# Feed-forward ends on Trainium2: weights prepared earlier, four row groups normalised by GpSimd, the last constant added by DMA

## The chip, the core and the metric

The kernel runs on one core of one Trainium2 chip. The metric is the device time of one launch in microseconds (us), lower is better. Instructions go to five engines that run side by side: PE (TensorE, matrix products), DVE (VectorE), ACT (ScalarE), POOL (GpSimd) and SP (SyncE, which only issues transfers). ACT and POOL can issue transfers as well. Every engine works through its own list in order, and waits for the others by semaphores.

## What is computed

The input x has 4096 rows of 256 numbers (C = 256), and adj is a 4096 x 4096 matrix of zeros and ones. Two layers follow one another; each adds an attention part and then a feed-forward part to x. The part that the change concerns is the first layer:

```
x = x + gat(layernorm(x), adj, W, a1, a2)       # 4 heads of 64, softmax over all 4096 columns where adj > 0, then elu
h = layernorm(x)
repeat 30 times:                                # the feed-forward
    h = h + 0.01 * tanh(h)
    h = h * sigmoid(h)
    h = layernorm(h) * ln_w + ln_b
    h = h @ W + b                               # W is 256 x 256
x = x + h
```

The second layer holds two more attention stages on the same adj, and then six experts, of which a router picks two for each row.

## The kernel before

**Stages.** The rows are cut into 32 tiles of 128, and 4 tiles make a row group of 512 rows (G = 4, so NG = 8 groups). The profile's span begins with the preparation of the first attention stage, g0 (0 to 95.6 us: projections of all rows, the weights of three stages, pieces of adj read and reduced to bytes). Its main loop follows (95.6 to 598), then the feed-forward (to about 1580), then the attention stages g1 and g2 (to 2682) and the experts.

**The attention loop.** It runs over 4 column chunks, 4 heads and 8 units: 128 units. For a unit, ACT and DVE make a sign tile `st` (L459, L461); DVE masks it in two instructions, `st` (L567) and `below` (L573), each on 128x1024 elements; PE accumulates products with both (L519). When a head is done, ACT copies one half of the sums into `lo` (`lower_sums`, L468), DVE adds the other half into `u` (`whole_sums`, L472), and `close` (L474 on) finishes it in small steps between the units of the next head: multiply, add, reciprocal (L482 to L494), an exponential into a tile `e` of its own (L497), and at last `finish` (L618), which adds the stage's input `old` (loaded by `begin`, L615) and stores 1024 rows of one head to `x1d` in DRAM (L624). So a row of x1d is complete when the last head of its chunk has been stored. In the first three chunks g0 also reads adj in 64 pieces of 1 MB through two buffers (`adj`, L200), makes bytes of them (L214) and transposes those by DMA (L217).

**The feed-forward.** 30 steps of 8 groups are 240 units. The loop body is `slot(at)`; one call holds pieces of several units, so the engines work on different units at once: for unit `at` the tanh (ACT, L826) and POOL's add `th + y` (L827); for unit at-2 the silu (L815), the split of its upper half in two 16-bit parts (ACT L817, DVE L818), their transposition by DMA on SP (L822), and row statistics (DVE L839); for unit at-3 PE's transposes of the lower half (L796), ACT's copy of them (L846) and 1/std (L849 on ACT, L850 and L851 on POOL); for unit at-4 the product `po` (PE, L863, L866); for unit at-5 the four DVE instructions (L803) that form the next `y`:

```python
nc.vector.scalar_tensor_tensor(
    y[:, g * G + r, :], po[:, r, :], rstd[:, r : r + 1],
    last if end else bias, op0=OP.mult, op1=OP.add,
)
```

The order of PE, DVE, ACT and POOL is the order in which the program is written here (a manual schedule); that of SP is made by the scheduler from times that it models. POOL's add of L827 is told to wait for L818 two units before[...].

**Its start.** The first values of y are the normalised rows of x1d. `load` fetches a group (`load_ahead`, L92; groups 0 to 3 through POOL's queue), `measure` takes statistics (DVE, L676 and L678), `rate` makes 1/std and the offset (ACT L684, POOL L685 to L688), and `init` writes y by four ACT instructions (L695). Groups 0 and 1 are prepared before the loop and the rest inside the first slots. Between them stands the preparation of the weights (L702 to L775): `ln_w` and `ln_b` are folded into W and b, W is centred, its range is found (`far`, L744 to L755), and it is written as `wT` (32 bit) and `w16` (two 16-bit parts), with the factors `scale` and `under`.

**Its end.** For the last step, units 232 to 239, the rows of x1d are loaded once more (L92 for groups 0 to 3, L790 for the others, issued from slot 228 on by the program, but placed early on SP). L803 adds `last` (the last step's bias with its factor undone) instead of `bias`; one slot later POOL adds the loaded rows (L877), and SP stores them to `x2d` (L878). Groups 0 to 3 stay in their buffers for the next stage, whose loads of the others follow on SP.

Of the kernel before, what the change touches and what calls it, by code (L numbers as in the profile page):

```python
# [11 lines left out]
F32 = mybir.dt.float32  # L12
BF16 = mybir.dt.bfloat16
F16 = mybir.dt.float16
# [9 lines left out]
P = 128  # L24
# [22 lines left out]
def gnn_ffn_kernel(ctx: ExitStack, tc: tile.TileContext, a: dict, out: bass.AP):  # L47
# [19 lines left out]
    ones = const.tile([2 * H, P], F32, name="ones")  # L67
    nc.gpsimd.memset(ones, 1.0)
# [19 lines left out]
    stream = []  # L88

    def load_ahead(src, g, view=rows_of, queue=nc.sync):  # L90
        t = stream[-1].tile([P, G, C], F32, name="rows")
        queue.dma_start(t, view(src, g))  # L92
        ahead[g] = t
# [67 lines left out]
    def attention(tag, src, norm, w, others, chunks, first, ends, following):  # L161
# [7 lines left out]
        with ExitStack() as scope:  # L169
# [26 lines left out]
            def load_piece(n):  # L196

                c, g, part = n // PER, n % PER // 4, n % 4
                i0 = c * CM * P + part * TR
                arow[n] = stream[-1].tile([P, 2, 8 * P], I32, name="adj")  # L200
                nc.sync.dma_start(
                    arow[n],
                    adj[i0 : i0 + TR, g * 8 * P : (g + 1) * 8 * P].rearrange("(p s) n -> p s n", s=2),
                )
# [28 lines left out]
            with ExitStack() as ps:  # L233
# [44 lines left out]
                def greatest():  # L278
# [8 lines left out]
                    nc.vector.tensor_scalar(dm, ident[: 2 * H, : 2 * H], fx, None, op0=OP.mult)  # L287
                    pt = small_ps()
                    nc.tensor.matmul(pt[:, : 2 * H], ones, dm, start=True, stop=True)
# [108 lines left out]
                for g in range(NG + 2):  # L398
# [19 lines left out]
                    if g in (3, 5) and late:  # L418
                        late.pop(0)()
# [56 lines left out]
            def close(c, h, u):  # L476
# [19 lines left out]
                e = end.tile([P, CM, D], F32, name="e")  # L496
# [40 lines left out]
            with tc.manual_schedule(engines={mybir.EngineType.DVE, mybir.EngineType.Activation}):  # L537
# [3 lines left out]
                for at in range(len(units) + LAG):  # L541
# [43 lines left out]
                    if first:  # L585
# [8 lines left out]
                        if at == len(units) - 30:  # L594
                            store_mask(len(chunks) * PER // 4 - 1)
                    if following and at == len(units) - 2 * following[0]:
                        for g in range(following[0]):
                            load_ahead(following[1], g, *following[2:])
# [7 lines left out]
    def to_rows(dst, src=None):  # L606
# [5 lines left out]
        def begin(t, n, h, work):  # L612
            if src is not None:
                old = work.tile([P, 8, D], F32, name="old")
# [20 lines left out]
    with tc.tile_pool(name="adj", bufs=2) as adjacency:  # L635
        stream.append(adjacency)
        attention("g0", x, True, w0, [make, *makers], [8, 8, 8, 8], True, to_rows(x1d, x), [])
    stream.append(ctx.enter_context(tc.tile_pool(name="stream", bufs=4)))
# [9 lines left out]
    with ExitStack() as scope:  # L648
        one = scope.enter_context(tc.tile_pool(name="f_one", bufs=1))
        wT = one.tile([P, C], F32, name="wT")  # L650
        w16 = one.tile([P, 2, C], F16, name="w16")
        scale = one.tile([P, 2], F32, name="scale")
        under = one.tile([P, 2, G], F32, name="under")
        eps = one.tile([P, 2], F32, name="eps")
        nc.gpsimd.memset(eps[:, :1], EPS)
        nc.gpsimd.memset(eps[:, 1:], EPS * 1e-4)
        bias = one.tile([P, C], F32, name="bias")
        last = one.tile([P, C], F32, name="last")
        y = one.tile([P, NT, C], F32, name="y")
        work = scope.enter_context(tc.tile_pool(name="f_work", bufs=3))  # L660
        small = scope.enter_context(tc.tile_pool(name="f_small", bufs=6))

        x1 = {}

        def load(g, queue=nc.sync):
            if g not in ahead:
                load_ahead(x1d, g, queue=queue)
            x1[g] = ahead.pop(g)

        measured, rates = {}, {}  # L670

        def measure(g):
            st = small.tile([P, G, 6], F32, name="x_st")
            mv = measured[g] = small.tile([P, G, 2], F32, name="x_mv")
            for r in range(G):
                nc.vector.bn_stats(st[:, r, :], x1[g][:, r, :])  # L676
            for r in range(G):
                nc.vector.bn_aggr(mv[:, r, :], st[:, r, :])  # L678

        def rate(g):  # L680

            mv = measured.pop(g)
            rs = small.tile([P, G], F32, name="x_rs")
            nc.scalar.activation(rs, mv[:, :, 1], AF.Identity, scale=1e-4, bias=eps[:, 1:])  # L684
            nc.gpsimd.tensor_tensor(rs, rs, mhalf, OP.pow)  # L685
            nm = small.tile([P, G], F32, name="x_nm")
            nc.gpsimd.tensor_tensor(nm, mv[:, :, 0], rs, OP.mult)
            nc.gpsimd.tensor_scalar(nm, nm, -1.0, None, op0=OP.mult)  # L688
            rates[g] = rs, nm
# [9 lines left out]
        for g in range(4):  # L699
            load(g, nc.gpsimd)  # L700
        with tc.tile_pool(name="f_prep", bufs=1) as prep, tc.tile_pool(name="f_pps", bufs=1, space=PSUM) as pps:
            ln = prep.tile([2 * KC, P], F32, name="ln")  # L702
            nc.scalar.dma_start(ln[:KC], a["L0_ffn_ln_w"].rearrange("(k p) -> k p", p=P))
            nc.scalar.dma_start(ln[KC:], a["L0_ffn_ln_b"].rearrange("(k p) -> k p", p=P))
            wr = prep.tile([P, KC, C], F32, name="wr")
            nc.scalar.dma_start(wr, a["L0_ffn_W"].rearrange("(k p) c -> p k c", p=P))
            nc.scalar.dma_start(bias, bcast_rows(a["L0_ffn_b"]))
            for g in range(3):
                measure(g)
                if g < 2:  # L710
                    rate(g)
            init(0)
            ps = pps.tile([P, 2 * KC], F32, name="ps_ln")
            nc.tensor.transpose(ps, ln, ident[: 2 * KC, : 2 * KC])
            lnT = prep.tile([P, 2 * KC], F32, name="lnT")
            nc.vector.tensor_scalar(lnT, ps, 100.0, None, op0=OP.mult)
            lbb = prep.tile([P, KC, P], F32, name="lbb")
            nc.vector.tensor_copy(lbb, lnT[:, KC:, None].to_broadcast([P, KC, P]))
            ps = pps.tile([P, KC, C], F32, name="ps_w")
            for k in range(KC):  # L720
                for o in range(KC):
                    nc.tensor.transpose(ps[:, k, o * P : (o + 1) * P], wr[:, o, k * P : (k + 1) * P], ident)
            raw = prep.tile([P, KC, C], F32, name="raw")
            nc.vector.tensor_copy(raw, ps)
            ps = pps.tile([P, C], F32, name="ps_b")
            for k in range(KC):
                nc.tensor.matmul(ps, lbb[:, k, :], raw[:, k, :], start=(k == 0), stop=(k == KC - 1))
            nc.vector.scalar_tensor_tensor(bias, bias, 100.0, ps, op0=OP.mult, op1=OP.add)

            nc.vector.tensor_scalar(last, bias, -100.0, 0.01, op0=OP.add, op1=OP.mult)  # L730
            for k in range(KC):
                nc.vector.tensor_scalar(raw[:, k, :], raw[:, k, :], lnT[:, k : k + 1], None, op0=OP.mult)
            ps = pps.tile([P, C], F32, name="ps_m")
            for k in range(KC):
                nc.tensor.matmul(ps, mean, raw[:, k, :], start=(k == 0), stop=(k == KC - 1))
            for k in range(KC):
                nc.vector.tensor_tensor(raw[:, k, :], raw[:, k, :], ps, OP.subtract)
            sq = prep.tile([P, KC, C], F32, name="sq")
            nc.vector.tensor_tensor(sq, raw, raw, OP.mult)
            ps = pps.tile([P, C], F32, name="ps_m")  # L740
            for k in range(KC):
                nc.tensor.matmul(ps, mean, sq[:, k, :], start=(k == 0), stop=(k == KC - 1))
            far = prep.tile([P, 4], F32, name="far")
            nc.vector.tensor_reduce(far[:, 0:1], ps, axis=AX.X, op=OP.max)  # L744
            nc.vector.tensor_scalar(far[:, 0:1], far[:, 0:1], TINY, None, op0=OP.add)
            nc.gpsimd.tensor_tensor(far[:, 1:2], far[:, 0:1], mhalf[:, :1], OP.pow)
            nc.vector.tensor_tensor(far[:, 1:2], far[:, 1:2], far[:, 0:1], OP.mult)
            nc.vector.tensor_reduce(far[:, 2:3], bias, axis=AX.X, op=OP.max, apply_absolute_value=True)
            big = prep.tile([P, 2], F32, name="big")
            nc.vector.tensor_scalar(big[:, 1:2], far[:, 1:2], math.sqrt(C), None, op0=OP.mult)  # L750
            nc.vector.scalar_tensor_tensor(
                far[:, 3:4], big[:, 1:2], math.sqrt(C), far[:, 2:3], op0=OP.mult, op1=OP.add
            )
            nc.vector.tensor_scalar(far[:, 3:4], far[:, 3:4], 0.01, 0.01, op0=OP.mult, op1=OP.add)
            nc.vector.tensor_scalar(big[:, :1], far[:, 3:4], math.sqrt(C) + 0.1, None, op0=OP.max)  # L755

            bits = prep.tile([P, 2], I32, name="bits")
            nc.vector.tensor_scalar(bits, big.bitcast(I32), 23, None, op0=OP.arith_shift_right)
            nc.vector.tensor_scalar(
# [620 lines left out]
```

## Time and profile before

| | before |
|---|---|
| median of 3 runs | 3018.31 us (3016.9 to 3024.39) |
| the profiled execution | 3008.46 us, of which its span 3006.8 us |
| busy in the span | PE 94%, DVE 91%, ACT 82%, POOL 39% |
| DMA queue of SP / of POOL, share of the 16 engines | 35.6% / 2.3% |
| PE's granted clock, mean | 0.974 |

Times of single instructions come from the profiled execution, counted from the start of its span. A busy share is an average over stages that have different limits, so it is read stage by stage. In the groups of instructions a row gives the line, engine, operation, tiles written and read, shape and count, then the total and mean duration, and last how long the engine stood idle before them and what ended that. In a timeline a bracket gives the idle time before an instruction and its releaser; SPq marks the issue of a transfer. A unit of g0's last chunk lasts 3.72 us, a head 29.8 us; a slot of the feed-forward's middle lasts 3.80 us.

### The profile page before, as it was taken

To read this page: it belongs to the slowest core of one execution; us is meant where nothing else is said; L and a number is where in the kernel's file an instruction comes from. 1 tells how busy PE (TensorE), PEld (TensorE's weight loads), DVE (VectorE), ACT (ScalarE), POOL (GpSimd) and SP (SyncE) were. 2 spreads that over 40 slices of the span, in tenths; PEclk is the share of its full clock that TensorE was granted. 3 is DMA by queue.
4 is the path that set the end of the run, shared out by engine and by line. 5 is a ranking of instruction groups with operands and counts; after the bars stand their busy time and mean duration, and the time that the engine had idled before them with its cause. 6 is when DMAs were issued, how large, how long until landed. Compare 5 with 4: busy or idle time off the path is not lost. (4 is left out here: it accounts for less than half of the span.)

```text
span 3006.8 us, 82646 instructions
## 1 busy us (share of the span) xinstructions
PE 2813.1 (94%) x33923; PEld 2568.3 (85%) x33923; DVE 2741.0 (91%) x5766; ACT 2462.0 (82%) x3132; POOL 1173.2 (39%) x1056
## 2 busy tenths in 40 slices
PE   6899999979999999999998999999889999986996
PEld 5799999958888888888876999999789999975996
DVE  8999999989999999999998899999689999986775
ACT  5799999788888888888866999999699999963442
POOL 2000000089999999999993000000200000013663
PEclk9999999989999999999999999999999999997998
DMA  9999784143333333333343031220303132133253
GB/s 292 267 256 249 224 247 118 33 133 70 68 68 67 68 70 69 68 68 68 68 95 121 20 103 51 76 79 27 107 20 93 51 107 79 51 96 123 82 172 134
DMA packets 482899, 320.08 MB, mean 106 GB/s; under 512 B 416573, under 2 KB 443354, under 8 KB 476378
## 3 DMA queue, kind: packets, MB, share of 16 engines
q1 hardware_dynamic: 467698, 287.13, 35.6%
q0 software_dynamic: 7680, 21.51, 2.3%
q10 hardware_dynamic: 7144, 6.16, 0.6%
q8 instruction: 268, 4.39, 0.6%
q14 instruction: 109, 0.89, 0.1%
HBM read 183.00 MB, written 52.04 MB: 78 GB/s over the span
## 5 line engine op out<-in xcount | busy, mean ns | idle before, releaser
L519 PE MATMUL acc<-vals,st 128*128 128x130 f16 x12288 | 1431.1, 218 | 36.1 <-DVE u L472 27.9
L519 PE MATMUL acc<-vals,below 128*128 128x130 f16 x12288 | 1430.7, 221 | 12.6 <-DVE below L573 11.9
L461 ACT ACTIVATE st<-f1b,nf 128x1024 int8<-128x1024 f32 x1265 | 1334.2, 1142 | 29.9 <-PE acc L519 24.6
L519 PEld LDWEIGHTS <-below 128*128 128x128 fp8e4 x12288 | 1175.7, 96 | 49.4 <-issue 44.5
L519 PEld LDWEIGHTS <-st 128*128 128x128 fp8e4 x12288 | 1207.5, 98 | 9.6 <-DVE st L567 7.5
L863 PE MATMUL po<-wT,zT 128*128 128x256 f32 x1920 | 576.1, 382 | 7.4 <-ACT zT L846 7.4
L827 POOL TENSOR_TENSOR th<-th,y 128x1024 f32<-128x1024 f32 x240 | 568.2, 2368 | 27.2 <-ACT th L826 4.4
L866 PE MATMUL po<-w,zT 128*128 128x256 f16 x3840 | 577.9, 273 | 0.3 <-DMA zT<-z 0.3
L866 PEld LDWEIGHTS <-zT 128*128 128x128 f16 x3840 | 376.3, 98 | 161.6 <-DMA zT<-z 1.2
L573 DVE TENSOR_TENSOR below<-m,st 128x1024 int32<-128x1024 int32 x384 | 470.0, 1224 | 32.8 <-DVE st L567 1.3
L567 DVE TENSOR_TENSOR st<-st,m 128x1024 int32<-128x1024 int32 x384 | 467.5, 1217 | 0.2
L803 DVE SCALAR_TENSOR_TENSOR y<-po,z_rs,bias 128x256 f32<-128x256 f32 x928 | 384.4, 477 | 2.1 <-PE tp L796 0.7
L839 DVE BATCH_NORM_STATS2 z_st<-z 128x6 f32<-128x256 f32 x960 | 335.8, 413 | 0.0
L863 PEld LDWEIGHTS po<-wT,zT 128*128 128x128 f32 x1920 | 291.1, 192 | 17.4 <-ACT zT L846 9.0
L105 POOL TENSOR_TENSOR ln_rstd<-ln_rstd,mhalf 128x4 f32<-128x4 f32 x24 | 32.3, 1345 | 586.5 <-ACT acc L1033 491.8
L815 ACT ACTIVATE z<-th 128x1024 f32<-128x1024 f32 x240 | 251.2, 1047 | 8.6 <-POOL th L827 8.3
L826 ACT ACTIVATE th<-y 128x1024 f32<-128x1024 f32 x240 | 249.8, 1041 | 0.1
L850 POOL TENSOR_TENSOR z_rs<-z_rs,mhalf 128x4 f32<-128x4 f32 x240 | 245.7, 1024 | 0.0
L846 ACT COPY zT<-tp 128x512 f32<-128x512 f32 x240 | 140.4, 585 | 110.5 <-PE tp L796 110.4
L459 DVE TENSOR_SCALAR st<-f1b,nf 128x1024 int8<-128x1024 f32 x271 | 201.2, 743 | 8.4 <-PE acc L519 8.4
L436 POOL MEMSET hs<- 128x4 f32 x3 | 0.3, 101 | 491.9 <-DVE u L489 491.9
L818 DVE SCALAR_TENSOR_TENSOR z<-z,scale,z 128x512 f16<-128x512 f32 x240 | 179.4, 747 | 4.9 <-ACT z L817 4.9
(252 smaller groups left out, 2970.2 us busy)
## 6 DMA issues: line engine op xcount, KB each, us to landing
adj<-in_adj_dram SPq DMA_DIRECT2D x64, 1024.0 KB
m<-edges SPq DMA_DIRECT2D x32, 1024.0 KB
f1b<-fd SPq DMA_DIRECT2D x48, 512.0 KB
edges<-m SPq DMA_DIRECT2D x16, 1024.0 KB
y<-yd SPq DMA_DIRECT2D x16, 512.0 KB
ew<-in_L_ffn_expert_w_dram SPq DMA_DIRECT2D x18, 256.0 KB
t<-in_x_dram SPq DMA_DIRECT2D x8, 512.0 KB
old<-in_x_dram SPq DMA_DIRECT2D x16, 256.0 KB
```

The lines of the kernel that those rows point to most:

```text
L461: nc.scalar.activation(out, f1, AF.Sign, bias=f2, scale=-1.0)
L519: nc.tensor.matmul(acc[:, i, cols], masked[part][:, at_i // TR, s, rows], v[:, cols], start=(j == 0 and part == 0), stop=(j == NT - 1 and ...
L567: nc.vector.tensor_tensor(above, above, whole, OP.bitwise_and)
L573: nc.vector.tensor_tensor(below, whole, above, OP.bitwise_xor)
L803: nc.vector.scalar_tensor_tensor(y[:, g * G + r, :], po[:, r, :], rstd[:, r : r + 1], last if end else bias, op0=OP.mult, op1=OP.add,)
L815: nc.scalar.activation(z, th.pop(u), AF.Silu, scale=0.01)
L826: nc.scalar.activation(th[at], y[:, g * G : (g + 1) * G, :], AF.Tanh, scale=0.01)
L827: ins = nc.gpsimd.tensor_tensor(th[at], th[at], y[:, g * G : (g + 1) * G, :], OP.add)
L839: nc.vector.bn_stats(st[:, r, :], z[:, r, :])
L850: nc.gpsimd.tensor_tensor(rs[u], rs[u], mhalf, OP.pow)
L863: nc.tensor.matmul(po[:, r, :], src[:, r * P : (r + 1) * P], wT, start=True, stop=False)
L866: nc.tensor.matmul(po[:, r, :], src16[:, part * G + r, :], w16[:, other, :], start=False, stop=(part == 1 and other == 1),)
```

## The change

**Weights.** Their preparation becomes two functions, `load_ffn` and `make_ffn`, called in g0's preparation beside those of g1 and g2 (`late`). The values are the same. Of the large steps, the copy of W, the two scalings by `ln_w`, the square and one half of `w16` go to ACT; two tiny ones go to POOL; the rest stays on DVE. PSUM results use the one small buffer that this preparation shares.

**Four groups early.** In g0's last chunk, 28 units before its end, SP loads groups 0 to 3. At 22, 18, 14 and 10 units before the end one group each is measured by DVE and normalised in place by POOL: `rs` and `nm` from five small instructions, then four of 128x256. The tanh and add of units 0 to 3 read that buffer, and only groups 4 to 7 go through `init`. The normalised rows of x1d are four more buffers' worth of data, so a `ring` of four row groups takes the place of both the adj pieces' buffers and the row groups' buffers, `e` is written into the free half of `u`, and `old` takes turns with `lo`.

**The last constant.** From slot 8 to slot 22 every second slot issues an accumulating transfer from POOL, which adds `last` to the 512 rows of one group of x1d in DRAM. The last step then adds `po * rstd` to the reloaded rows in one go and stores them from there, so L877 and the second use of y disappear.

```diff
-    stream = []
+    ring = keep.tile([P, 4, G, C], F32, name="ring")
+    turns = [0]
     def load_ahead(src, g, view=rows_of, queue=nc.sync):
-        t = stream[-1].tile([P, G, C], F32, name="rows")
+        t = ring[:, turns[0] % 4]
+        turns[0] += 1
         queue.dma_start(t, view(src, g))
...
-                arow[n] = stream[-1].tile([P, 2, 8 * P], I32, name="adj")
+                arow[n] = ring[:, 2 * (n % 2) : 2 * (n % 2) + 2].rearrange("p s r c -> p s (r c)").bitcast(I32)
...
-                    if g in (3, 5) and late:
+                    if g in (3, 5, 6) and late:
                         late.pop(0)()
...
-                e = end.tile([P, CM, D], F32, name="e")
+                e = u[:, :, 1, :D]
...
+                    if len(units) - at in side:
+                        side[len(units) - at]()
...
-                old = work.tile([P, 8, D], F32, name="old")
+                old = work.tile([P, 4, 2, DV], F32, name="old", tag="lo", bufs=2)
...
+    def init_early(g):
+        rate(g, True)
+        rs, nm = rates.pop(g)
+        for r in range(G):
+            nc.gpsimd.tensor_scalar(
+                x1[g][:, r, :], x1[g][:, r, :], rs[:, r : r + 1], nm[:, r : r + 1], op0=OP.mult, op1=OP.add
+            )
+    EARLY = 4
+    def early_loads():
+        for g in range(EARLY):
+            load(g)
+    def early_rows(g):
+        measure(g)
+        init_early(g)
+    side = {28: early_loads, **{22 - 4 * g: functools.partial(early_rows, g) for g in range(EARLY)}}
+    attention("g0", x, True, w0, [make, *makers, (load_ffn, make_ffn)], [8, 8, 8, 8], True, to_rows(x1d, x), [], side)
...
-        for g in range(4):
-            load(g, nc.gpsimd)
-        with tc.tile_pool(name="f_prep", bufs=1) as prep, tc.tile_pool(name="f_pps", bufs=1, space=PSUM) as pps:
...
-            for g in range(3):
-                measure(g)
-                if g < 2:
-                    rate(g)
-            init(0)
...
         def slot(at):
-            if 0 < at and at + 3 < NG:
+            if 0 < at and EARLY <= at + 3 < NG:
                 load(at + 3)
...
+                t = x1.pop(g) if end else None
                 for r in range(G):
                     nc.vector.scalar_tensor_tensor(
-                        y[:, g * G + r, :],
+                        t[:, r, :] if end else y[:, g * G + r, :],
                         po[:, r, :],
                         rstd[:, r : r + 1],
-                        last if end else bias,
+                        t[:, r, :] if end else bias,
...
+                if end:
+                    nc.sync.dma_start(rows_of(x2d, g), t)
+                    if g < NG // 2:
+                        ahead[g] = t
...
-                nc.scalar.activation(th[at], y[:, g * G : (g + 1) * G, :], AF.Tanh, scale=0.01)
-                ins = nc.gpsimd.tensor_tensor(th[at], th[at], y[:, g * G : (g + 1) * G, :], OP.add)
+                was = x1.pop(at) if at < EARLY else y[:, g * G : (g + 1) * G, :]
+                nc.scalar.activation(th[at], was, AF.Tanh, scale=0.01)
+                ins = nc.gpsimd.tensor_tensor(th[at], th[at], was, OP.add)
...
+            if NG <= at < 3 * NG and at % 2 == 0:
+                nc.gpsimd.dma_start(
+                    rows_of(x1d, (at - NG) // 2), last[:, None, :].to_broadcast([P, G, C]), accum_op=OP.add
+                )
...
-                nc.gpsimd.tensor_tensor(t, t, y[:, g * G : (g + 1) * G, :], OP.add)
-                nc.sync.dma_start(rows_of(x2d, g), t)
```

## The prediction

> **What bounds the kernel now.** First the busy time by stage, because the change touches four places: the first attention stage's preparation (30 to 95 us), its last column chunk (480 to 598), the feed-forward's start (600 to 650) and its end (1540 to 1590). Columns are busy time and instructions of PE, PEld, DVE, ACT and POOL, then the granted clock, the DMA share and GB/s.
>
> ```profile
> 30.00:95.00 65.00, 47.73 (x219) 37.82 (x217) 61.69 (x113) 49.13 (x73) 23.61 (x36) 0.95 0.98 289
> 480.00:560.00 80.00, 79.39 (x1376) 79.15 (x1373) 75.59 (x85) 74.56 (x76) 0.00 (x0) 1.00 0.18 58
> 600.00:650.00 50.00, 28.47 (x143) 20.20 (x144) 39.92 (x133) 41.45 (x73) 36.75 (x43) 0.73 0.58 167
> 650.00:850.00 200.00, 200.00 (x1431) 163.79 (x1429) 199.39 (x667) 175.88 (x260) 191.58 (x155) 1.00 0.35 69
> 1540.00:1590.00 50.00, 42.53 (x271) 33.13 (x271) 42.03 (x144) 21.88 (x35) 45.07 (x35) 0.97 0.46 134
> ```
>
> The preparation is bound by DVE (61.69 of 65), the last chunk by PE (79.39 of 80). The feed-forward's middle has PE and DVE both full and POOL 8.4 us short of full in 53 slots, 0.16 us a slot. Only start and end have holes. The waits of 660 to 1540 us confirm the middle; no transfer is in their list:
>
> ```profile
> ACT zT L846 <- PE tp L796: 107.4, 222, 0.5
> ```
>
> Next the timeline of the start (start, duration, engine, line):
>
> ```profile
> 609.73 2.34 POOL L827 TENSOR_TENSOR th<-th,y 128x1024 f32<-128x1024 f32 x1 [2.80 <-ACT th L826]
> 609.80 2.82 DVE L739 TENSOR_TENSOR sq<-raw 128x512 f32<-128x512 f32 x1
> ...
> 616.03 2.34 POOL L827 TENSOR_TENSOR th<-th,y 128x1024 f32<-128x1024 f32 x1
> 616.10 2.29 DVE L747 TENSOR_TENSOR far<-far 128x1 f32<-128x1 f32 x1 [0.70 <-POOL far L746]
> 616.23 1.28 ACT L815 ACT_TABLE_LOAD   x1
> 617.53 1.06 ACT L815 ACTIVATE z<-th 128x1024 f32<-128x1024 f32 x1
> ...
> 620.44 0.72 ACT L817 ACTIVATE z<-z,scale 128x512 f16<-128x512 f32 x1 [1.86 <-DVE inv L763]
> ```
>
> The weight chain ends in `scale`, for which ACT waits 1.86 us; afterwards each slot holds one `init` of four 0.588 us activations, and the silus come every 5.47 us (624.17, 629.64, 635.11, 640.58) where the middle's slot takes 3.80. The end, first POOL, then SP:
>
> ```profile
> 1576.78 2.35 POOL L877 TENSOR_TENSOR x<-x,y 128x1024 f32<-128x1024 f32 x1
> 1579.09 1.02 POOL L105 TENSOR_TENSOR ln_rstd<-ln_rstd,mhalf 128x4 f32<-128x4 f32 x1
> 1580.08 2.35 POOL L877 TENSOR_TENSOR x<-x,y 128x1024 f32<-128x1024 f32 x1
> ```
>
> ```profile
> 1575.60 7.21 SPq L878 DMA_DIRECT2D x2d<-x  x3
> 1582.98 0.39 SPq L92 DMA_DIRECT2D rows<-x2d  x1
> ```
>
> Eight adds at L877 go through POOL, and the load of a row group for the next stage stands on SP behind stores that wait for them.
>
> **What the Trainium skill says.** *SBUF — State Buffer*, "Who interferes with whom": a DVE instruction with two SBUF inputs and a GpSimd instruction that reads SBUF share a port pair, and the later one is fully blocked. The trace agrees: L739 and L747 above end with POOL's add, at 2.82 and 2.29 us. *DMA: Bandwidth & Descriptors*, "SWDGE vs HWDGE vs iDMA": accumulating in a transfer is possible from GpSimd only. No run here shows it; its nearest rows are GpSimd's plain loads. "Anatomy of one DMA" there: a semaphore wait is served by the issuing sequencer, not by the DMA engines. So a waiting load holds back everything behind it on SP.
>
> **The change, part by part** (us; plus is slower).
>
> *Start.* POOL's finished rows let tanh of groups 0 to 3 begin without `init`. Before, silu(5) began at 645.86. After, the first tanh (1.04) follows the old DVE tail (last store issued at 606.39) much as now, but the table load no longer waits for the weights, and four of the eight 5.47 us slots become 3.80: 4 x 1.67 = 6.7, plus 4.8 for the weight waits and blocked DVE instructions ahead of silu(0) (2.82 - 0.6, 2.29 - 0.15, and part of the 1.86). **-11.5**, between -8 and -14. Groups 4 to 7 still run `init` on ACT, each ahead of its tanh.
>
> *Weights into the preparation.* Some 4.2 us of DVE work, by the durations of the same lines now (STT 0.42, subtracts 0.75, two reduces 0.84, w16 0.45, wT 0.38, nine tiny ones near 0.15), in a stretch where DVE has 5% idle: **+4**. Copy, scales and square go to ACT, 2.3 us, hidden behind DVE (ACT 49.13 of 65). Six more users of the one small PSUM buffer serialise with the other preparations: 2 to 9 in all.
>
> *Four groups in the last chunk.* Statistics are 4 x 1.57 us of DVE (one instruction is 408 ns) at units 106, 110, 114 and 118 of 128, so two each in heads 1 and 2. POOL adds 16 rows of 128x256; the nearest row is POOL's copy of that shape, 0.40, so each can block an `st`/`below` (1.22 us, two SBUF inputs) by up to 0.4: 16 x 0.4 x 0.8 = 5. The lines that carry the cover:
>
> ```profile
> L676 DVE BATCH_NORM_STATS2 x_st<-rows 128x6 f32<-128x256 f32 x15 | 5.4, 408 | 0.0
> L472 DVE TENSOR_TENSOR u<-acc,lo 128x520 f32<-128x520 f32 x7 | 4.9, 698 | 3.1 <-ACT lo L468 3.1
> ```
>
> DVE's only idle time here is 3.1 us before L472, about 1.27 a head. Demand is 6.3 + 5.2 = 11.5; two heads' idle takes 2.5, and DVE's lead over PE (2.6 to 4.9 us) about 3. **+6**; 0 without contention, +12 with twice of it. The statistics at 590 to 599 leave the old place, but there they hid behind the last head's tail. The loads leave POOL (3.77 us of issue at 474.6, hidden in idle time) for SP at 28 units from the end, 100 us ahead of their use: 0.
>
> *Store before sums.* `e` now lives in `u`, so L472 of the next head waits until the last head's store has landed. Gaps from the store's issue to L472 are 3.5 to 5.9 us now; a quiet store lands 2.15 after its issue (606.39 to 608.54), a loaded one later. Chunks 0 to 2 have twelve heads at a DMA share of 0.88: **+2**, between 0 and 10. `old` in `lo`'s buffers puts its load behind L472 on SP, and piece transposes behind that; DVE is two or more units ahead of them, 0.
>
> *Accumulates.* Eight, one in every second slot from 8 to 22. On POOL each costs an issue, 0.95 by the four plain ones: 0.8 in two slots more than the 0.32 idle there; 8 x 0.6 = 5 if nothing else stalls. On SP it is worse. In the changed program the load of group k for the last step waits for accumulate k, and stands ahead of the transposes of units 8+2k and 9+2k; the old ones had been issued by 646. The plain POOL row:
>
> ```profile
> rows<-x1d POOLq DMA_DIRECT2D x4, 512.0 KB, 6.0
> ```
>
> POOL issues accumulate k about 1 us after L818 of unit 7+2k (L827 waits for that, then pow and product). At 6.0 to land, SP is released at +7. The transpose of unit 8+2k was due at 3.80 + 0.75 = 4.55: 2.4 late, plus 0.4 of issue and 1 to 1.6 behind a 512 KB load in its own queue, less the slack of 1.9 between a transpose's landing (3.75) and its matmuls: 2.7. A stall delays the neighbours too, so every second accumulate then passes: 4 x 2.7 = 11. After the end's 2.59 us PE stall, matmul groups took 1.06 instead of 0.60 for 3.5 us, at a granted clock of 0.90; 1.2 for each stall makes 5. It covers the POOL excess. **+16**; 2 if the accumulate lands in 4 us, 28 if in 8 with every one stalling.
>
> *End.* Gone are eight adds of 2.35 and the path sum, add, store, load. PE's last `po` ended at 1579.3 where 3.8 us slots give 1573.4: 5.9, plus some of the 3.10 us that DVE waits for rows<-x2d until 1587.27. **-6.5**, between -3 and -9. The last sums then read `t` in place, the same four 0.477 us instructions.
>
> Sum: -11.5 + 4 + 6 + 2 + 16 - 6.5 = **+10**. The profiled execution took 3008.46 (span 3006.8), so 3018.5 by its clock; the median of the runs stands 9.85 above, and the forecast is on that footing: 3018.31 + 10 = 3028.
>
> **The rivals.** *The ends pay* (faster). If an accumulate lands within 4 us of its issue, SP is free by the time the transpose is due, and POOL's rows are as short as 0.3 us. Then -11.5 + 4 + 2 + 0 + 1 - 6.5 = -11, about 3007. It decides at a landing of 4.2; for it speaks that indirect POOL transfers of 128 KB land in 2.4 to 2.9, against it that the only 512 KB ones took 5.3 to 6.7 (in a busier DMA stretch) and that an accumulate reads its destination as well. *Everything waits*: landings of 8 us and blocked DVE work of twice my value, -10 + 5 + 12 + 4 + 26 - 5 = +32, 3050. For it: the clock drop after each stall. *It doesn't do what it says*: the start is set by the old attention tail and by the 1.28 us table load, not by weights and `init`. Then the start gains 5 and the stalls are half: -5 + 4 + 3 + 1 + 7 - 6 = +4, 3022.
>
> **How the numbers follow.** A difference of 0.3% (9 us) is about what a measurement of this kernel can tell. Forecast (+3 to +20) 0.48, ends pay (-18 to -4) 0.32, everything waits (+20 to +40) 0.16, little happens 0.04. Faster by 9: three quarters or so of the second, 0.25. Slower by 9: 0.6 of the first and all of the third, 0.46. The rest, 0.29. The range, 3002 to 3046, leaves some 0.08 out at each side; the likeliest case alone is 3021 to 3038.
>
> **What would show it.** Right: in the waits of 660 to 730 us, PE or PEld waits for zT<-z, two or three us each, about four times, and SP waits for an accumulate to land; silus of the first slots near 3.8 apart; `st` and `below` above 1.22 in units 106 to 120; no L877; L92 of group 4 before 1580 less the shift. Wrong: accumulates landing below 4 us with no PE wait (the ends pay), or the preparation's first L519 still at 95.6.

## The result, and the profile after

The median went from 3018.47 us (8 runs) to 3029.45 us (8 runs): the ratio is 1.0032, with a 95% interval of 1.0021 to 1.0043. The profiled execution took 3024.71 us, its span 3023.0. The busy time by stage, columns as in the prediction (busy time of PE, PEld, DVE, ACT, POOL, granted clock, DMA share, GB/s):

```profile
30.00:95.00 65.00, 53.26 (x263) 42.79 (x262) 61.89 (x133) 52.95 (x82) 27.08 (x42) 1.00 0.99 284
600.00:650.00 50.00, 31.57 (x293) 25.70 (x291) 38.57 (x108) 33.57 (x55) 29.51 (x29) 0.83 0.37 85
650.00:850.00 200.00, 188.26 (x1315) 151.43 (x1313) 187.53 (x616) 162.34 (x238) 186.78 (x150) 0.98 0.62 105
1540.00:1590.00 50.00, 50.00 (x358) 40.77 (x357) 49.96 (x173) 33.65 (x52) 41.35 (x38) 1.00 0.58 129
```

PE lost 11.7 of the 200 us between 650 and 850, where it had been full, while the DMA share nearly doubled. The waits of 660 to 760 us, where the list of before held little but ACT's wait for PE (the others were 0.4 us each), and below it those of SP from 600 to 760 (waiting engine and line, what for, us, times, longest):

```profile
PEld L898 <- DMA zT<-z: 15.2, 9, 3.4
PE po L898 <- DMA zT<-z: 11.7, 8, 3.0
DVE y L826 <- PE po L898: 10.3, 7, 3.3
POOL th L855 <- DVE z L845: 6.6, 5, 2.6
```

```profile
SPq L812 <- DMA x1d<-last: 21.6, 4, 8.0
SPq L92 <- DMA x1d<-last: 21.3, 4, 6.1
```

SP waits 43 us for the eight accumulates, and PE gets the transposes behind them late. One of them in the timelines of POOL and of SP (start, duration, engine, line):

```profile
656.45 1.57 POOL L887 DMA_DIRECT2D x1d<-last  x1
```

```profile
663.74 0.36 SPq L92 DMA_DIRECT2D ring<-x1d  x1
664.27 3.47 SPq L849 DMA_TRANSPOSE zT<-z  x2
```

The issue takes POOL 1.57 us (the median of the eight is 1.33), SP is released 7.3 us after it began, and the transpose of unit 8 follows only then.

From such timelines the table below compares the lengths of the stages, in us against a second profile of the kernel before (first row, absolute ends of the stages). "Weights" is up to g0's first product, "chunks 0-2" up to the first product of the last chunk, "last chunk" up to g0's last product, "silu(0)" from g0's last product to the first silu, "u8" to the lower half's instruction (L818, later L845) of unit 8, "u29" and "u220" to that of units 29 and 220, "po" to the end of the feed-forward's last product; "g1 prep" and "g2 prep" up to the first product of that stage and "loop" from there to its last; the last column is the sum up to g2's last product.

| | weights | chunks 0-2 | last chunk | silu(0) | u8 | u29 | u220 | po | g1 prep | g1 loop | g2 prep | g2 loop | sum |
|---|---|---|---|---|---|---|---|---|---|---|---|---|---|
| before, us | 95.6 | 478.8 | 598.2 | 617.6 | 659.1 | 740.8 | 1489.5 | 1579.5 | 1644.2 | 2129.5 | 2193.6 | 2678.8 | |
| before, first profile | 0.0 | 0.0 | 0.0 | 0.0 | 0.0 | 0.0 | 0.0 | 0.0 | +0.1 | +1.5 | +0.7 | +0.5 | +2.9 |
| after | +4.1 | 0.0 | +7.3 | -11.5 | +0.4 | +16.3 | 0.0 | -5.8 | -5.0 | +2.3 | +0.5 | +2.2 | +10.8 |
| e1_sp_order | +5.2 | +1.1 | +5.8 | -11.5 | +0.9 | +13.5 | +19.7 | -4.1 | -5.1 | +2.0 | +0.3 | +2.0 | +29.8 |
| e2_no_accum | +4.8 | +2.1 | +7.3 | -11.5 | +4.3 | 0.0 | 0.0 | -5.8 | -3.0 | +2.0 | +0.5 | +3.3 | +3.9 |
| e3_scratch | +4.8 | +4.0 | +5.8 | -11.5 | +4.8 | +12.9 | +19.6 | -4.1 | -5.1 | +2.4 | +0.4 | +3.1 | +37.0 |
| e4_old_end | +6.0 | +4.1 | +5.8 | -11.5 | +4.8 | 0.0 | 0.0 | +0.7 | +0.1 | +3.2 | +1.1 | +1.9 | +16.1 |
| e5_rows_late | +4.9 | +3.7 | +2.3 | -4.3 | -1.8 | +16.0 | 0.0 | -5.8 | -4.1 | +1.9 | +0.6 | +2.3 | +15.6 |
| e6_bn_only | +5.2 | +0.4 | +7.5 | -11.5 | +0.6 | +18.3 | 0.0 | -5.8 | -4.9 | +2.6 | -0.6 | +2.0 | +13.7 |
| e8_weights_late | +1.6 | +2.2 | +5.8 | +5.0 | +0.3 | +13.6 | 0.0 | -5.8 | -3.9 | +2.8 | +0.7 | +3.2 | +25.6 |
| e10_early_acc_spread | +4.7 | +4.2 | +4.1 | -11.5 | +4.5 | +2.9 | +20.4 | -4.6 | -5.0 | +2.4 | +0.6 | +2.3 | +24.8 |
| e11_one | +5.3 | +2.0 | +7.4 | -11.5 | +2.1 | +1.9 | 0.0 | -5.8 | -2.9 | +2.1 | +0.3 | +2.2 | +2.9 |
| e12_one_issue | +5.1 | +5.6 | +4.1 | -11.5 | +1.3 | +11.2 | 0.0 | -5.8 | -5.2 | +1.9 | +1.0 | +1.9 | +9.4 |
| e13_share | +0.8 | +2.6 | +1.6 | +0.1 | 0.0 | 0.0 | 0.0 | 0.0 | -1.1 | +1.9 | -0.7 | +2.6 | +7.7 |

The two profiles of before agree to 0.03 us up to the end of the feed-forward. From unit 29 to unit 220 a slot of before lasts 3.92 us; the 3.80 given ahead for the middle hold for the first units, up to 13. Behind g2 lie the experts, where of the change only one shared buffer for tables of index numbers runs: they took 325.1 and 335.4 us in the two profiles of before, 333.4 after, and 320 to 338 over all. So their difference in a single pair of profiles says nothing, and total times of one run are not used below. The sum of +10.8 up to there stands beside the +11.0 of the medians, but such a sum compares one profile with one: for e4_old_end it is +16.1 where the medians differ by 11.2, for e12_one_issue +9.4 where they differ by 3.5. So the stages are read one by one.

### The profile page after: what moved, and what is told of

It is laid out like the page before. It is cut to its first block, busy times and chain, and to the rows that moved or that the text cites. A ratio compares the mean times of both kernels' runs of the same rounds, so it can differ in the third digit from the quotient of the medians.

```text
span 3023.0 us, 82652 instructions
## 1 busy us (share of the span) xinstructions
PE 2807.8 (93%) x33923; PEld 2562.4 (85%) x33923; DVE 2738.8 (91%) x5756; ACT 2458.1 (81%) x3117; POOL 1206.8 (40%) x1075
## 5 line engine op out<-in xcount | busy, mean ns | idle before, releaser
L519 PEld LDWEIGHTS <-st 128*128 128x128 fp8e4 x12288 | 1208.3, 98 | 11.5 <-DVE st L567 8.9
L898 PE MATMUL po<-w,zT 128*128 128x256 f16 x3840 | 579.0, 274 | 11.7 <-DMA zT<-z 11.7
L898 PEld LDWEIGHTS <-zT 128*128 128x128 f16 x3840 | 376.3, 98 | 175.5 <-DMA zT<-z 15.2
L895 PEld LDWEIGHTS po<-wT,zT 128*128 128x128 f32 x1920 | 291.6, 192 | 15.2 <-ACT zT L874 6.7
L845 DVE SCALAR_TENSOR_TENSOR z<-z,scale,z 128x512 f16<-128x512 f32 x240 | 182.3, 760 | 3.2 <-ACT z L844 3.2
```

Of the source, the lines that this page charges most:

```text
L519: nc.tensor.matmul(acc[:, i, cols], masked[part][:, at_i // TR, s, rows], v[:, cols], start=(j == 0 and part == 0), stop=(j == NT - 1 and ...
L895: nc.tensor.matmul(po[:, r, :], src[:, r * P : (r + 1) * P], wT, start=True, stop=False)
L898: nc.tensor.matmul(po[:, r, :], src16[:, part * G + r, :], w16[:, other, :], start=False, stop=(part == 1 and other == 1),)
```

## The experiments

In the experiments' kernels a line number can be a few off that of the changed kernel; the tiles tell the instruction.

**What the accumulates cost.** Three kernels take away SP's wait, the accumulates themselves, or only the dependence. In e1_sp_order SP follows the program's order, so the reloads stand at slots 228 to 235:

```diff
                 mybir.EngineType.Pool,
+                mybir.EngineType.SP,
```

> SP is put into the manual schedule, so that the eight loads of the last step stand in the order of the program, at slots 228 to 235, where their accumulates landed long ago. Theory A (the transposes are held behind loads that wait for accumulates): the stretch from the lower half's instruction (L845) of unit 8 to that of unit 29, 98.0 us in the changed kernel and 81.7 in the kernel before, falls to 82 to 86, PE waits for zT vanish, and the median falls by 12 to 16 to about 3015. Theory B (POOL's longer issue, 1.33 us each, and its late adds cost the time): the stretch stays above 92 and the median falls by less than 6.

e2_no_accum leaves the eight transfers out; e3_scratch sends them elsewhere:

```diff
-                    rows_of(x1d, (at - NG) // 2), last[:, None, :].to_broadcast([P, G, C]), accum_op=OP.add
+                    rows_of(x1s, (at - NG) // 2), last[:, None, :].to_broadcast([P, G, C]), accum_op=OP.add
```

> The eight accumulates are left out, so the last constant is missing from the output. Both theories: the stretch from unit 8 to unit 29 is that of before, 81.7; po of unit 239 ends about 16 us earlier than in the changed kernel (1590.2), near 1574. It is the zero for the next kernel.

> The eight accumulates are issued as in the changed kernel, but into a tensor of their own that nothing reads (the last constant is missing from the output), so no load waits for them. POOL's issue and the DMA traffic stay, SP's wait is gone. Theory A: the stretch is 82 to 86. Theory B: 92 to 98.

Without accumulates the stretch from unit 8 to unit 29 takes 81.7 us again, so all 16.3 are theirs. The feed-forward's last product ended at 1580.6 us, though, 9.8 earlier than in the changed kernel and not 16: the stretch up to unit 8 was 3.9 longer. That comes from SP's order. In e2, e3 and e4, where no load waits for an accumulate, the scheduler put the load of group 4 behind g0's last store, 10.9 us after g0's last product instead of 7.2, and its statistics waited. The waits of 608 to 670 us, first in the changed kernel, then in e2_no_accum:

```profile
DVE x_st L735 <- DMA ring<-x1d: 1.7, 3, 0.7
```

```profile
DVE x_st L735 <- DMA ring<-x1d: 5.0, 1, 5.0
```

But without SP's wait it still takes 13.5 (e1) and 12.9 (e3) more than before, and then each later slot takes 4.02 us instead of 3.92 right up to the end, another 19.7. The medians say the same: e1_sp_order was slower than before by a ratio of 1.0105 (1.0087 to 1.0124). Theory A, the prediction's, falls as the only cause, and B understates. The waits of e1_sp_order from 810 to 1500 us:

```profile
ACT z L842 <- POOL th L855: 102.1, 171, 0.7
PEld L898 <- DMA zT<-z: 3.1, 4, 1.2
```

POOL is now the engine that all wait for, long after the last accumulate. What differs is seen by laying the timelines of two slots side by side, POOL and DVE, first of before (its second profile), then of e10_early_acc_spread, which is just as slow:

```profile
1000.43 2.37 POOL L827 TENSOR_TENSOR th<-th,y 128x1024 f32<-128x1024 f32 x1
1002.75 1.02 POOL L850 TENSOR_TENSOR z_rs<-z_rs,mhalf 128x4 f32<-128x4 f32 x1
1003.86 0.41 POOL L851 TENSOR_TENSOR z_rs<-z_rs,under 128x4 f32<-128x4 f32 x1
```

```profile
1003.47 0.74 DVE L818 SCALAR_TENSOR_TENSOR z<-z,scale,z 128x512 f16<-128x512 f32 x1
```

```profile
1001.34 2.37 POOL L863 TENSOR_TENSOR th<-th,y 128x1024 f32<-128x1024 f32 x1
1003.67 1.47 POOL L886 TENSOR_TENSOR z_rs<-z_rs,mhalf 128x4 f32<-128x4 f32 x1
1005.21 0.20 POOL L887 TENSOR_TENSOR z_rs<-z_rs,under 128x4 f32<-128x4 f32 x1
```

```profile
1003.29 0.96 DVE L853 SCALAR_TENSOR_TENSOR z<-z,scale,z 128x512 f16<-128x512 f32 x1
```

Before, DVE's instruction with two SBUF inputs falls behind POOL's add and ahead of its short product. In the other case POOL is about 1.1 us later in the slot, counted from DVE's instruction: its add still runs when DVE's instruction begins, which is then longer (0.96 for 0.74), and the pow that follows the add falls into that instruction and takes 1.47 for 1.02. This agrees with the shared port pair that the prediction took from the Trainium skill's page *SBUF — State Buffer*, "Who interferes with whom". POOL's three instructions and the gaps then fill 4.02 us, and the loop keeps this **second rhythm**. From 900 to 1300 us POOL is busy for 392 of 400 us in it, against 383 before. That the lack of idle time is what keeps it there is argued, not tested.

What leads into it was tried with one accumulate only, SP in program order:

```diff
-            if NG <= at < 3 * NG and at % 2 == 0:
+            if at == NG:
```

> SP in the manual schedule as in e1_sp_order, but only the accumulate of slot 8 is left (the last constant is missing from seven row groups of the output). Theory C (the loop has two rhythms; one issue on POOL pushes POOL's pow under DVE's two-input instruction L845, and the loop stays there): from unit 40 to unit 220 a slot takes 4.02 us, the pow about 1.47 us instead of 1.02, and po of unit 239 ends about 19 us late, although only one transfer was issued. Theory D (the slow rhythm needs the repeated pushes, or an order of SP): 3.92 and 1.02; the one issue costs 1 to 2 us.

The one push cost 3 us in all (1.1 between units 6 and 8, 1.9 after), more than D's 1 to 2, and the loop came back to 3.92: D holds, C falls. Two things follow: the slow rhythm takes repeated pushes, and it can be left again. What separates the runs is DVE. In all that came back (the changed kernel, e11 and, described below, e5, e6, e8 and e12) a transpose held PE up, and DVE then waited for PE's product, 2.1 to 13.9 us in all; in the three that stayed slow (e1, e3 and, below, e10) no wait of DVE for PE is listed from 655 to 1560 us. POOL then had to wait for DVE's L845 in five of the six (6.6 us in the changed kernel), in e8 not at all. DVE's timeline in e8 shows the step (L847 there is L845 of the changed kernel):

```profile
748.51 0.94 DVE L847 SCALAR_TENSOR_TENSOR z<-z,scale,z 128x512 f16<-128x512 f32 x1
752.16 1.66 DVE L828 SCALAR_TENSOR_TENSOR y<-po,z_rs,bias 128x256 f32<-128x256 f32 x4 [1.11 <-PE po L900]
753.74 0.74 DVE L847 SCALAR_TENSOR_TENSOR z<-z,scale,z 128x512 f16<-128x512 f32 x1
```

The wait moves DVE's instruction back in relation to POOL; it takes 0.74 again, and every slot from there on 3.92 or close to it. So the stalls of the changed kernel seem to have spared it the 19.7 us. This fits all runs; no run holds the transposes back on purpose, so it is argued and not shown.

**Accumulates out of the loop.** In a candidate, groups 0 to 3 get theirs in g0's last chunk, the others in slots 3 to 6, and the early groups are spread over the four heads:

```diff
-    side = {28: early_loads, **{22 - 4 * g: functools.partial(early_rows, g) for g in range(EARLY)}}
+    side = {28: early_loads, **{26 - 7 * g: functools.partial(early_rows, g) for g in range(EARLY)}}
...
     def early_rows(g, pool):
         measure(g)
+        add_last(lasts[0], g)
...
+            if 3 <= at < 3 + NG - EARLY:
+                add_last(last, at - 3 + EARLY)
```

> A candidate: SP in the manual schedule; the accumulates of groups 0 to 3 in g0's last chunk, where POOL is idle, those of groups 4 to 7 in slots 3 to 6, which ACT's init makes 5.5 us long; the four groups measured at 26, 19, 12 and 5 units before the end, so one in each head. Theory C: no accumulate falls in the steady loop, so a slot takes 3.92, the stretch from unit 8 to 29 is 81.7; against the kernel before, preparation +4 to +6, last chunk +2 to +6, start -11.5, end -5.8 and g1's preparation -5: 8 to 14 us faster than before, ratio about 0.996. If POOL is pushed in slots 3 to 6 and does not recover, a slot takes 4.02 and the kernel is 5 to 12 us slower than before.

It was slower: 1.0074 (1.0060 to 1.0088) against before. The four in slots 3 to 6 were enough to lead into the second rhythm (4.02 us a slot, +20.4 up to unit 220). This also shows that the slow rhythm needs no accumulate near it. The spread made the statistics cheaper: behind its first 128 products the last chunk was 2.5 us longer than before, where the changed kernel's was 5.7. So the four were made one transfer of 2 MB at slot 8:

```diff
-            if 3 <= at < 3 + NG - EARLY:
-                add_last(last, at - 3 + EARLY)
+            if at == NG:
+                nc.gpsimd.dma_start(
+                    x1d[EARLY * GR :, :].rearrange("(r p) c -> p r c", p=P),
+                    last[:, None, :].to_broadcast([P, (NG - EARLY) * G, C]), accum_op=OP.add)
```

> As e10_early_acc_spread, but groups 4 to 7 get the constant from a single accumulating transfer of 2 MB at slot 8 instead of four in slots 3 to 6. Theory C (two rhythms, and only repeated pushes lead into the slow one): slots of 3.92 from unit 40 on, the one push costs 1 to 4, po of unit 239 ends near 1579 as before, and the median lies within 6 us of the kernel before. If an issue of four times the rows takes POOL four times as long (5 us), the push costs 5 or more, or the loop enters the slow rhythm (4.02, +19 us).

The issue took 2.18 us, not four times as long, and the loop came back to 3.92. The push cost about 2 us (two slots of 5.58 and 4.02 instead of 3.80); the rest of the loss is one slot of 12.73 us, in which a transpose was late. The timeline of PE's weight loads:

```profile
678.19 0.56 PEld L908 LDWEIGHTS <-zT 128*128 128x128 f16 x4 [8.50 <-DMA zT<-z]
```

SP waits for no transfer here. While the 2 MB ran, the DMA share was 1.1 to 1.2 (665 to 680 us; 0.26 from 645 to 655), and the issues of the transposes on SP, 1.23 us each otherwise, took 2.9, 5.1 and 2.4 us in a row; PE waited 8.5 us, and its granted clock was 0.60 from 680 to 685. That the transfer held up the transposes is read from this coincidence. Stretch u29: +11.2. The candidate's ratio to before is 1.0014 (1.0007 to 1.0022): nearer to it than the changed kernel's 1.0032, and not faster. No complete version that was run beats the kernel before. So an accumulate can cost in three places: POOL's time, the transfers beside it, and what waits for it.

**The end alone.**

```diff
-                    t[:, r, :] if end else bias,
+                    last if end else bias,
...
+                nc.gpsimd.tensor_tensor(t, t, y[:, g * G : (g + 1) * G, :], OP.add)
+                nc.sync.dma_start(rows_of(x2d, g), t)
```

> The changed kernel with the old end: no accumulates, the adds of L877 on POOL again. If the parts add up (preparation +4.1, last chunk +5.5, start -9.4, all kept; accumulates +16.3 and end -5.9 gone), po of unit 239 ends near 1579.7 against 1579.3 before, and the median is that of before within 3 us, about 3019. If the end's gain was not the adds' (but the earlier load, or the ring), po of unit 239 still ends 37.5 us or less after the lower half of unit 231 and the median falls to about 3013.

po is 0.7 late and g1's preparation 0.1, against -5.8 and -5.0: both gains belong to the end. The rest did not go as expected: the feed-forward's last product ended at 1589.4 us, and the ratio is 1.0036 (1.0026 to 1.0045). The expectation had left out the loops of g1 and g2 (+5 together), and two stages were longer than in the changed kernel: chunks 0 to 2 (+4.1 for 0.0) and the stretch to unit 8 (+4.8 for +0.4). The second is the late load of group 4, as in e2_no_accum. Why chunks 0 to 2 vary from 0.0 to +5.6 among kernels that share this code is left open.

**The start alone.**

```diff
-    EARLY = 4
+    EARLY = 0
...
+        for g in range(4):
+            load(g, nc.gpsimd)
+        for g in range(3):
+            measure(g)
...
+        init(0)
```

> The changed kernel without the four early groups: loads from POOL's queue, statistics, rate and init in the feed-forward's first slots as before; weights stay early, accumulates stay. From the last product of g0 to silu(0) it takes 19.39 us before and 7.86 after. Theory A (weights and rows share the gain): 13 to 15, because tanh(0) then starts where it did before, 10.4 after the last product, and add and table load follow. Theory B (the weights alone): about 8. Theory C (the rows alone): about 19. The last chunk is 5 to 7 us shorter than after, and silus stay 5.3 to 5.5 apart up to unit 6.

From the last product to silu(0): 15.1 us, at the edge of theory A; 19.4 before and 7.9 after. Early weights bring 4.3, early rows 7.2 more, taken in this order. The last chunk kept +2.3 although nothing of the rows was left in it.

In e8_weights_late `make_ffn` is called after g0's loop instead:

> The changed kernel with the weights prepared after g0's loop, as before, by the new function. If the preparation pays for them on DVE, g0's first product comes 4 us earlier than in the other runs of this group. From g0's last product to silu(0): theory A 12 to 16, since silu needs no weights but its 16-bit split does; the rest is waited for in the split of unit 0 then, until some 20 after the last product.

The weights' column falls to +1.6, 2.5 under the changed kernel and 3 to 4 under most others: about 3 us are the weights', the rest is not explained by them. The second expectation missed. Silu(0) came 24.4 us after the last product, 5 later than before: five steps of the new function that run on ACT (copy, two scalings, square, half of w16, from 615.8 to 628.0) stand ahead of tanh(0) on it and wait for DVE and PE in turn.

**The last chunk.** In e6_bn_only `init_early(g)` is left out of `early_rows`:

> The changed kernel with the statistics of the four groups in the last chunk, but without POOL's normalisation of them (the feed-forward starts from rows that are not normalised). The last chunk was 5.8 to 7.3 us longer than before. Theory A (DVE's own 4 x 1.75 us): it is still 5 or more longer. Theory B (the port that DVE and POOL share): under 3 longer, and st and below never above 1.25 us.

The chunk is as long as with POOL's work (+7.5 against +7.3), so theory A holds and B falls. In both, 1.6 of it is a lower clock at the beginning of the chunk (below, under the shared buffers); the statistics make the rest, 5.9 here and 5.7 in the changed kernel. The groups of DVE from 483 to 610 us, first with POOL's work (the changed kernel), then without:

```profile
L573 DVE TENSOR_TENSOR below<-m,st 128x1024 int32<-128x1024 int32 x31 | 38.7, 1247 | 2.6
L567 DVE TENSOR_TENSOR st<-st,m 128x1024 int32<-128x1024 int32 x31 | 38.0, 1227 | 0.0
L735 DVE BATCH_NORM_STATS2 x_st<-ring 128x6 f32<-128x256 f32 x16 | 5.6, 410 | 0.0
```

```profile
L573 DVE TENSOR_TENSOR below<-m,st 128x1024 int32<-128x1024 int32 x32 | 39.2, 1224 | 2.7
L567 DVE TENSOR_TENSOR st<-st,m 128x1024 int32<-128x1024 int32 x31 | 37.7, 1218 | 0.0
```

The mean of `below` rises by 23 ns and that of `st` by 9: 1 us in 62 instructions. POOL paid instead:

```profile
L757 POOL TENSOR_SCALAR ring<-ring,x_rs,x_nm 128x256 f32<-128x256 f32 x16 | 24.9, 1567 | 0.4
```

A row took 1.57 us there; the same shape as a POOL instruction by itself (`last` at the feed-forward's start, L785) took 0.41.

**The shared buffers.** The remaining +2.3 of e5_rows_late in the last chunk, and +2 in each of the loops of g1 and g2, were laid to `e` in `u` and `old` in `lo`. e13_share is the kernel before with only that:

```diff
-                e = end.tile([P, CM, D], F32, name="e")
+                e = u[:, :, 1, :D]
...
-                old = work.tile([P, 8, D], F32, name="old")
+                old = work.tile([P, 4, 2, DV], F32, name="old", tag="lo", bufs=2)
```

> The kernel before with the sharing of buffers alone: e in the free half of u, old in turn with lo. Theory E (L472 of a new head waits for the last head's store to land, and that costs where PE bounds): g0's last chunk 2 to 2.5 us longer than before, the loops of g1 and g2 2 us longer each, DVE waits at L472 for x1d<-u, h1d<-u and x3d<-u; all else within 0.5, the DMA-bound chunks 0 to 2 of g0 within 0 to 4. Rival: the sharing costs nothing, and those microseconds are from the ring or from the code's place in the schedule: all within 0.5.

Last chunk +1.6, g1 +1.9, g2 +2.6: these are near the sizes of theory E (preparation +0.8 and g1's preparation -1.1 lie outside its 0.5). Its mechanism is there in g1 and g2. The waits of 1700 to 2690 us, first before (second profile, which has none for a store), then e13_share:

```profile
PE acc L519 <- DVE u L472: 8.8, 29, 0.3
```

```profile
PE acc L519 <- DVE u L472: 11.8, 29, 1.1
DVE u L472 <- DMA h1d<-u: 11.0, 4, 5.6
...
DVE u L472 <- DMA x3d<-u: 4.2, 3, 1.9
```

L472 of a new head waits for a store of the last one to land, where before it waited for ACT alone, and PE waits 3.0 us longer for it in the two loops. The other 1.5 us are no more than what g1's loop varied by in the two profiles of before.

In the last chunk no L472 waits for a store. The difference lies in its first 128 products, which took 8.95 us instead of 7.37; all products after them took 112.0 us in both kernels. The first 9 us of the last chunk in before, e1_sp_order and e13_share (columns as above):

```profile
478.70:487.70 9.00, 8.95 (x156) 8.95 (x156) 8.86 (x10) 8.62 (x9) 0.00 (x0) 1.00 0.87 310
485.10:494.10 9.00, 9.00 (x157) 9.00 (x157) 8.86 (x10) 8.61 (x9) 0.00 (x0) 1.00 0.64 220
482.10:491.10 9.00, 8.96 (x129) 8.96 (x129) 8.86 (x10) 7.32 (x7) 0.00 (x0) 0.81 0.98 332
```

PE was as busy and did fewer products, at a granted clock of 0.81 instead of 1.00. Ahead of these products PE had stood still for the same 2.49 us in all three. The changed kernel, e2, e6 and e11 have the 0.81 too; e1, e3, e4 and e8, which share the same buffers, have 1.00 and a last chunk of +5.8; in e5_rows_late, after a stall of 4.3 us, it was 0.73, and that is its whole +2.3. So theory E falls for the last chunk. What decides between the two clocks is left open.

The second profile of the experts again:

> The kernel before once more, for a second profile of it on the chip of this group of runs. If the 8.3 us by which the experts' part (from the last product of g2 to the end) was longer in the changed kernel's profile is an effect of the change, it takes 325 here; if it is from run to run, anything from 318 to 335.

It took 335.4, and 325.1 in the first: from run to run.

## Why the prediction was right, and where it was right for the wrong reason

The time (3028 forecast, 3029.45 measured) and the sum (+10, +10.8 up to g2's end) came out. Term by term:

- **Weights, +4**: +4.1; the other kernels with the same preparation stand at 4.7 to 6.0. e8_weights_late returns 2.5 of it.
- **Last chunk, +6**: +7.3, of which 1.6 is the lower clock at its beginning and 5.7 the statistics. The working failed in its split. DVE's idle time and its lead over PE were to hide 5.5 of the 6.3 us of statistics, and POOL's rows were to add 5.2 by blocking `st` and `below`. Nearly nothing was hidden (5.9 without POOL's work), and the blocking made 1 us of DVE time that lengthened nothing, since POOL was the one that waited (1.57 us a row instead of the 0.40 taken). The two errors cancelled: luck.
- **Store before sums, +2 in chunks 0 to 2**: 0.0 here, 0.4 to 5.6 in the other kernels that share the buffers, so the runs neither confirm the term nor refute it. With the sharing alone (e13_share, +2.6) one L472 waited 1.4 us for a store, but PE waited no longer for L472 from 97 to 478 us (15.2 us against 15.4), and ran at a clock of 0.91 instead of 1.00 in the fourth head (196 to 229 us). Where the wait did cost, in g1 and g2, the prediction had put nothing: their loops are 2.3 and 2.2 longer, and in e13_share 3.0 of 4.5 are that wait. The stores it waited for let it begin 4.8 to 5.6 us after their issue, not 2.15.
- **Start, -11.5**: -11.5 to silu(0). But the step "four of the eight 5.47 us slots become 3.80" failed: from the lower half of unit 0 to that of unit 6 it took 29.3 us, 29.8 before, and the silus came 5.3 to 7.1 apart up to unit 5. In a slot with `at` = u + 2 stand the silu of unit u and the `init` of group u + 3, so the 5.47 us slots of the silus 1 to 4 are those of groups 4 to 7, which kept their `init`; the freed ones lie ahead. Besides, ACT waited 3.2 us for x_mv L737 between 600 and 660 us. The whole gain lies ahead of silu(0), in the old tail, weights and rows: 19.4 became 7.9.

```profile
616.19 1.28 ACT L842 ACT_TABLE_LOAD   x1
617.49 1.06 ACT L842 ACTIVATE z<-th 128x1024 f32<-128x1024 f32 x1
618.58 0.72 ACT L844 ACTIVATE z<-z,scale 128x512 f16<-128x512 f32 x1
...
622.73 0.30 ACT L746 ACTIVATE x_rs<-x_mv,eps 128x4 f32<-128x4 f32 x1 [2.48 <-DVE x_mv L737]
```

  The split of unit 0 (L844) follows its silu without a wait now, and ACT then waits for the statistics of group 4.
- **Accumulates, +16**: +16.3. The held transposes are there: PE waited 11.7 us in eight waits of up to 3.0, where four of 2.7 were forecast (the figures given there add up to 1.9 to 2.6); the landing was 6.1 to 7.8, median 6.6, in e3_scratch, against the 6.0 taken. Two of the waits were followed by matmul groups of 1.06 us instead of 0.60; by their starts that makes some 3 us, an estimate, where 5 were set. But the step that set POOL's share beside it at "5 if nothing else stalls" was mis-sized: without SP's wait POOL and the transfers cost 12.9 to 13.5, the issue being 1.33 and not 0.95, and the pow in this stretch taking 1.37 (after) and 1.68 us (e1_sp_order) instead of 1.02. The second rhythm was not foreseen at all.
- **End, -6.5**: -5.8 at po, as worked out there (5.9), and -5.0 more in g1's preparation, where the share of the earlier load had been set at 0.6 by taking the term as -6.5. DVE's wait for group 4's rows fell from 3.10 to 0.55, which is half of the 5.0; the other half is not taken apart:

```profile
1592.18 1.37 DVE L100 BATCH_NORM_STATS2 ln_st<-ring 128x6 f32<-128x256 f32 x4
1595.30 1.41 DVE L100 BATCH_NORM_STATS2 ln_st<-ring 128x6 f32<-128x256 f32 x4 [0.55 <-DMA ring<-x2d]
```

The missed gain of the end (4.3) and what the sum had left out from g1's loop to the end of g2's (5.0) cancelled; that the total came out is luck to that extent. Two of the signs named for "right" did not come: silus 3.8 apart in the first slots, and `st` and `below` clearly above 1.22. One reading was loose: L739 ended 0.55 us after POOL's add, L747 with it.

The rival "the ends pay" fell at its own point: it needed landings below 4.2. "It doesn't do what it says" fell with the start, which gained 11.5 and not 5. "Everything waits" did not come either: the clock fell after two of the eight stalls only, and was 0.98 in 650 to 850 us, 0.96 in 655 to 740.

## What to carry to other kernels

In a loop whose engines are all nearly full, cost a new instruction by the idle time of its own engine in that slot and by where it pushes what follows it: a short issue on GpSimd moved its next instructions under a DVE instruction on the shared port, and the loop could stay in that slower rhythm for 180 slots. A buffer that is saved by sharing turns "was read" into "has landed" for the next writer, so look for the price in the stages where that writer stands on the path, not in the one that the change is about. Before a microsecond is put down to a wait, read the granted clock of that stretch. A sum that comes out right is no proof of its terms; compare the stages one by one.

## What the runs showed of the hardware beyond that

The same loop ran steadily at two rates, 3.92 and 4.02 us a slot, with the same instructions and the same order on each engine. A GpSimd transfer of 512 KB that accumulates took 1.33 us to issue and one of 2 MB 2.18, against 0.95 for plain ones of 512 KB; the landing of the 512 KB ones, 6.6 us, was hardly longer than that of the plain ones (6.0). After the same 2.49 us of standing still, PE went on at a granted clock of 1.00 for 9 us in six profiles (both of before among them) and at 0.81 in five.
